# Two-layer spatial CNN scan: another order of two late phases, with new queues for their transfers, and shorter hand-overs from row scans to column scans

## The chip, the cores and the metric

The kernel runs on one core of a Trainium2 chip. A core has TensorE (PE, matmuls), VectorE (DVE), ScalarE (ACT), GpSimd (POOL) and SyncE (SP), which work from queues of their own, and 16 DMA engines that move data between DRAM and on-chip memory (SBUF). DMAs are issued from SP's, ScalarE's or GpSimd's queue. The metric is the time of one execution in microseconds.

## The reference

The input `x` is 32 images of 48 channels, 64 rows and 128 columns, float32. Two layers follow each other, each with its own weights; a layer normalizes, scans in four directions and adds the result to its input:

```python
def f(carry, inp):                    # one scan step; w: 48 x 48 x 5 taps
    nxt = inp + _conv1d(carry, w, b)  # convolution along the line
    return (nxt, nxt)
...
# down over the 64 rows, then up, then right over the 128 columns, then left,
# each direction on the output of the one before
...
x = x + _L0_conv_ref(_gn(x), ...)     # _gn: group norm, 16 groups of channels
x = x + _L1_conv_ref(_gn(x), ...)
```

The down and up scans use the same weights. Every step needs the step before, so a scan over rows is a chain of 63 steps in each direction, and one over columns a chain of 127.

## The kernel before, in words

The 32 images are four groups of 8 (`GB`). Row scans take one group at a time, column scans a pair of groups. So there are twelve phases, in the order of the tuple `PHASES`: `("rows", layer, group)` is a down and an up scan, `("cols", layer, pair)` a right and a left scan. The trace names the matmuls of a scan by layer, number and direction: `step_01u` is layer 0, group 1, up; `step_10r` is layer 1, pair 0, right. This text uses the same names. Before, layer 1 ends with the rows of groups 1, 2 and 3, then the columns of pair 0, then those of pair 1.

A step (`step`, matmuls at L741, VectorE's at L750) is 9 float32 matmuls into PSUM, and 3 VectorE instructions that add the bias and the step's input line and write the new line into SBUF, where the next step's matmuls read it.

SBUF holds three slots. A row phase has its 64 rows in them in two halves (`row_views`). A column phase has four quarters of 32 columns each, which share the slots (`slots`, `quarter`): the first is written out to `spill` after the right scan has passed it and the fourth takes its place; the left scan gets it back later. A quarter is six units (`UNITS`): three blocks of channels times the two groups of the pair. The scans' layouts differ, rows with whole lines in the free dimension and columns with blocks of 8 rows or columns (`E8`), so between them data pass through DRAM, in `ups`, called `upa` for layer 0 and `upb` for layer 1 in the trace.

What surrounds the steps is an agenda: `at(t, fn, ...)` puts a function at a step number, and the functions are traced in the order of these numbers. `in_order` keeps each engine's instructions in that order; nothing else paces them, so a transfer leaves as soon as its queue reaches it and what it waits for is done. `t0` is a phase's first step, `left` the start of its left scan, `end` its last step. The parts that matter here:

- `move_rows` writes finished rows to `ups` in blocks of 8 rows, ten DMAs for each (L231 is the common line of all DMAs), and loads a row phase's input from `source` (`mid` for layer 1) in four chunks of 16 rows, 20 DMAs each, on SP's queue. `scale_rows` (L614) then applies the normalization to a chunk with 24 ScalarE activations.
- `follows(k)` says that a column phase starts right after the rows of the second group of its own pair. Before, that holds for pairs 0 and 1 of layer 0. At such a seam the first quarter's units of that group are loaded on GpSimd's queue in pieces as its rows become ready: the blocks of rows from 32 on, then 16 to 31, 8 to 15, and at last rows 0 to 7. `move_rows` cuts the last block into rows 2 to 7 and rows 0 and 1. `hold_queues` makes SP's queue (by a tiny DMA into `pin`) and ScalarE's (by a copy) wait for the second column, before they load the second quarter.
- In the left scan each unit of a finished quarter goes through `load_residual`, `add_residual` (GpSimd, L673), for layer 1 `permute_unit` (L698, 3 copies on GpSimd and 5 on ScalarE for one unit), and then out. Layer 1's residual loads are on ScalarE's queue, into four tiles of `stage` and, for pair 0, one spare tile.
- Pair 1 of layer 1, the last phase, stores its results into `out` with `store_result`. So does pair 0 with the fourth quarter. The quarters named in `HELD` go to DRAM tiles `held` as one large DMA per unit instead (`hold_result`), and `let_result` copies them from there to `out` during the last phase, DRAM to DRAM, 48 results in 60 DMAs, on SP's queue.

The lines of the agenda that set the results' hand-over and the residual loads' queue, before:

```python
at(end + 63 + 1.9 * n, let_result, *what)
...
dma(nat[p0 : p0 + c1 - c0], by_col(t, e, j)[c0:c1], nc.scalar if layer else None)
```

Of the kernel before, what the change touches and what calls it, by code (L numbers as in the profile page):

```python
# [29 lines left out]
F32 = mybir.dt.float32  # L30
# [12 lines left out]
GB = 8  # L43
E8 = 8
FULL = 128
NG = E8 * C // FULL
NQ = 4
# [3 lines left out]
PIECES = (  # L51
    (0, 0, 48, 0, 0),
    (1, 0, 48, 0, 48),
    (2, 0, 32, 0, 96),
    (2, 32, 48, 1, 0),
    (3, 0, 48, 1, 16),
    (4, 0, 48, 1, 64),
    (5, 0, 16, 1, 112),
    (6, 0, 48, 2, 0),
# [19 lines left out]
def weight_runs():  # L79
# [24 lines left out]
PHASES = (  # L104
    ("rows", 0, 0),
    ("rows", 0, 1),
    ("cols", 0, 0),
    ("rows", 0, 2),
    ("rows", 1, 0),
    ("rows", 0, 3),  # L110
    ("cols", 0, 1),
    ("rows", 1, 1),
    ("rows", 1, 2),
    ("rows", 1, 3),
    ("cols", 1, 0),
    ("cols", 1, 1),
)

# [2 lines left out]
def kernel(  # L121
# [8 lines left out]
    nc = tc.nc  # L130
    B, _, H, W = x.shape
    NK = W // E8
    NH = H // E8
    KQ = NK // NQ
    WQ = W // NQ
    N = NK * GB
    RUN = KQ * GB
# [5 lines left out]
    BN = 512  # L143
# [8 lines left out]
    dram = ctx.enter_context(tc.tile_pool(name="dram", bufs=1, space=bass.MemoryType.DRAM))  # L152
# [19 lines left out]
    spare_tiles = [early[:, i * UNIT : (i + 1) * UNIT] for i in range(2)]  # L172
# [12 lines left out]
    junk = early[:, 3 * WEIGHTS + NG * N :]  # L185
# [15 lines left out]
        dram.tile([2 * NG, FULL, UNIT], F32, tag=f"spill{i}", name=f"spill{i}")  # L201
        for i in range(4)
    ]
    pin = dram.tile([FULL, 1], F32, tag="pin", name="pin")


    HELD = (2, 1, 0)
    held = {
        (j, half): dram.tile([NG, FULL, UNIT], F32, tag=f"held{j}{half}", name=f"held{j}{half}")
        for j in HELD  # L210
        for half in range(2)
    }

    def by_row(t, e, h0, h1):


        t = t.rearrange("c (i q a e n) -> e a c i q n", i=E8, q=NQ, a=NH, e=E8)[e, h0 // E8]
        return t[:, h0 % E8 : h0 % E8 + h1 - h0].rearrange("c i q n -> c (i q) n")

    def lines(t, h0, h1):  # L220

# [3 lines left out]
    def by_col(t, e, j):  # L225


        return t.rearrange("c (i q n) -> i q c n", i=E8, q=NQ)[e, j]

    def dma(dst, src, queue=None):  # L230
        (queue or nc.sync).dma_start(dst, src)  # L231

    tail = {}

    def in_order(fn, *args):


        traced = nc.cur_bb.bb.instructions
        n = len(traced)
        fn(*args)  # L240
        for ins in traced[n:]:
            if ins.engine in tail:
                tc.add_manual_dep(
                    ins,
                    tail[ins.engine].name,
                    mybir.DependencyInfo(
                        mybir.DependencyClass.NoSync, mybir.DependencyReason.DATA
                    ),
                    reason="in_order",
                )  # L250
            tail[ins.engine] = ins

    def pieces(o):
# [332 lines left out]
    def row(k, h):  # L586
        return row_views(k)[h // HALF][:, :, h % HALF]

    def move_rows(k, h0, h1, to_dram):

        _, layer, g = PHASES[k]
        view = row_views(k)[h0 // HALF]
        t = (ups if to_dram else source)[layer][g]
        for h in range(h0, h1, E8):
            end = min(h1, h + E8)
            for o in range(NG):
                for e, c0, c1, p0 in pieces(o):
                    here = view[p0 : p0 + c1 - c0, o, h % HALF : h % HALF + end - h]
                    here = here.rearrange("p h (q n) -> p (h q) n", q=NQ)
                    there = by_row(t, e, h, end)[c0:c1]  # L600
                    if to_dram:
                        dma(there, here)
                    else:
                        dma(here, there)
# [23 lines left out]
    UNITS = [(g, half) for g in range(NG) for half in range(2)]  # L628

    def quarter(k, j):  # L630
        return slot[slots(k)[j % 3]].rearrange("p (o s n) -> p s o n", s=2, o=NG)
# [13 lines left out]
                queue,  # L645
            )

    def hold_queues(k):

        done = quarter(k, 0)[:, 0, 0, RUN : RUN + 1]  # L650
        dma(pin, done)
        nc.scalar.copy(junk[:, BN - 1 :], done)

    def spill_unit(k, i, back):
        _, layer, pair = PHASES[k]
# [7 lines left out]
    def load_residual(k, j, i, nat):  # L663
        _, layer, pair = PHASES[k]
        o, half = UNITS[i]
        t = source[layer][2 * pair + half]
        for e, c0, c1, p0 in pieces(o):
            dma(nat[p0 : p0 + c1 - c0], by_col(t, e, j)[c0:c1], nc.scalar if layer else None)

    def add_residual(k, j, i, nat, eng=nc.gpsimd):  # L670
        o, half = UNITS[i]
# [28 lines left out]
    def in_output(j, g, e):  # L700


        t = out[g * GB : (g + 1) * GB].rearrange("b c (a e) w -> e (c a) b w", e=E8)
        return t[e, :, :, j * WQ : (j + 1) * WQ]
# [9 lines left out]

    def hold_result(j, i, perm):
        o, half = UNITS[i]
        dma(held[j, half][o], perm, nc.scalar)

    def let_result(j, half, e):

        src = held[j, half].rearrange("o p (a b n) -> (o p a) b n", a=NH, b=GB)
        for n, c0, c1, g, p0 in PIECES:
            if n == e:
                at = (g * FULL + p0) * NH
                dma(in_output(j, half, e)[c0 * NH : c1 * NH], src[at : at + (c1 - c0) * NH])


    def step(key, weights, b_at, src, inp, dst, whole, part):
# [91 lines left out]
    def at(t, fn, *args):  # L820
        agenda.append((t, len(agenda), fn, args))
# [31 lines left out]
    def plan_rows(k, t0, prev):  # L853
        if k == 1:
            ahead, scaled = (-34, -18, -3, 12), (-12, -2, 17, 33)
        elif prev == "cols":
            ahead, scaled = (-28, -12, 4, 20), (-13, 3, 19, 35)
        else:
            ahead, scaled = (-54, -43, 0, 11), (-22, -8, 16, 30)
        if k:  # L860
            for i in range(4):
                at(t0 + ahead[i], move_rows, k, i * LOAD, (i + 1) * LOAD, False)
                at(t0 + scaled[i], scale_rows, k, i * LOAD, (i + 1) * LOAD)

        cuts = list(range(0, H + 1, E8))
        following = PHASES[k + 1][0] == "cols"
        if following and follows(k + 1):
            cuts = [0, E8 // 4] + cuts[1:]
        for h0, h1 in zip(cuts, cuts[1:]):
            t = t0 + 2 * (H - 1) - h0  # L870
            if k == 0:
                t += 16 if h0 >= HALF else 68
            elif not following:
                t = t0 + 92 + 5 * (H - h1) / E8 + (34 if h1 <= HALF else 0)
            at(t, move_rows, k, h0, h1, True)
        at(
            t0 + H - 1,
            nc.gpsimd.tensor_copy,
            last.rearrange("p (o n) -> p o n", o=NG),
            row(k, H - 1),  # L880
        )

    def follows(k):

        _, layer, pair = PHASES[k]
        return PHASES[k - 1] == ("rows", layer, 2 * pair + 1)

    def plan_cols(k, t0, prev):
        _, layer, pair = PHASES[k]
        n = 2 * NG  # L890
        after = prev == "cols"
        if follows(k):
            at(t0 + 1.2, hold_queues, k)
        for i in range(n):
            if follows(k) and UNITS[i][1] == 1:
                other = nc.gpsimd
                at(t0 - 31 + i, load_unit, k, 0, i, 4, NH, 0, E8, other)
                at(t0 - 13 + i, load_unit, k, 0, i, 2, 4, 0, E8, other)
                at(t0 - 6 + i / n, load_unit, k, 0, i, 1, 2, 0, E8, other)
                at(t0 - 1.5, load_unit, k, 0, i, 0, 1, E8 // 4, E8, other)  # L900
                at(t0, load_unit, k, 0, i, 0, 1, 0, E8 // 4, other)
            else:
                early = 30 if after else 46 if k == 2 else 70
                at(t0 - early + 2 * i, load_unit, k, 0, i)
            if follows(k):
                queue = nc.scalar if i % 2 else nc.sync
                at(t0 + 1.5, load_unit, k, 1, i, 0, NH, 0, E8, queue)
            else:
                at(t0 + (3 if after else -24 + 2 * i), load_unit, k, 1, i)
            at(t0 + (38 if after else 8) + 2 * i, load_unit, k, 2, i)  # L910
            at(t0 + 33 + 2 * i, spill_unit, k, i, False)
            at(t0 + 50 + 2 * i, load_unit, k, 3, i)
        final = k == len(PHASES) - 1
        left = t0 + W - 1
        end = left + W - 1
        for i in range(n):

            t = left + 64 + 2 * i if layer == 0 else left + 39.5 + 4.5 * i
# [8 lines left out]
        if layer == 0:  # L927
            stats = ResultStatsV(f"r{2 * pair}"), ResultStatsA(f"r{2 * pair + 1}")
        tiles = [stage[:, i] for i in range(4)]
        if layer:  # L930
            tiles += spare_tiles[0 : 2 if final else 1]
        n = len(tiles)
        direct = [u for u in units if not (final and u[1] == 0)]

        for u, (t, j, i) in enumerate(direct):
            nat = tiles[u % n]
            o, half = UNITS[i]
# [26 lines left out]
        if layer == 0:  # L964
            t = units[-1][0] + 14
# [6 lines left out]
        if layer and not final:  # L972
            todo = [(j, half, e) for j in HELD for half in range(2) for e in range(E8)]
            for n, what in enumerate(todo):
                at(end + 63 + 1.9 * n, let_result, *what)
        if final:
            at(end + 4, last_results, k)

# [23 lines left out]
    tiles = [stage[0:PX, i] for i in range(4)]  # L1002
# [140 lines left out]
    done = 0  # L1143
# [65 lines left out]
```

## Time and profile before

| | us |
|---|---|
| median of three runs | 4292.32 (4289.52 to 4297.63) |
| the profiled execution | 4290.3 |
| its span in the profile | 4288.2 |
| TensorE busy | 4058.9 (95%) |
| VectorE busy | 2164.5 (50%) |
| ScalarE busy | 1340.1 (31%) |
| GpSimd busy | 886.2 (21%) |
| first step of a scan | 107.8 |
| last step of a scan ends | 4207.7 |
| granted TensorE clock, mean | 0.981 |

The profile is one execution, taken apart: busy time by engine, 40 slices of the span, the waits of each engine with what ended them, the timeline of instructions and of DMA issues, and windows, which give every engine's busy time in a stretch together with TensorE's granted clock (1.00 is full speed), the mean busy share of the 16 DMA engines and the rate in GB/s. Times in the profile count from the start of the span. A queue's name ends in q: SPq is SP's DMA queue. A row of a DMA queue shows when the issues ran, not when the data landed; the landing is given apart, as a time from issue.

### The profile page before, as it was taken

The numbers are of one execution on the slowest core, as the hardware profiler recorded it, in microseconds if no ns is written. First come the engines' busy times: TensorE is split into PE (matmuls) and PEld (weight loads), VectorE is DVE, ScalarE is ACT, GpSimd is POOL, SyncE is SP. The second block draws the span as 40 slices with busy tenths as digits, with TensorE's granted clock in tenths as the row PEclk, the third lists the DMA queues.
The fourth block names the chain that finished last, engine by engine and source line by source line (L and its number), as shares of the span: only waits on it lengthen the run. The fifth ranks groups of instructions, "written<-read, shape, count | busy, mean of one in ns | idle before, by whom it ended". The sixth has DMA issues, their size and how long they took to land. (4 is left out here: it accounts for less than half of the span.)

```text
span 4288.2 us, 89979 instructions
## 1 busy us (share of the span) xinstructions
PE 4058.9 (95%) x36648; PEld 4029.3 (94%) x36648; DVE 2164.5 (50%) x6503; ACT 1340.1 (31%) x2662; POOL 886.2 (21%) x906
## 2 busy tenths in 40 slices
PE   3699998999999999998999999999999999999992
PEld 1699998999999999998999999999999999999992
DVE  6345444446664444444446654444444444444443
ACT  1584301435793564100006772613000002210122
POOL 4271001325323020010005310000000024510352
PEclk9899999999999999999999999999999999999996
DMA  9599799857998979679308979939289049999999
GB/s 213 113 216 162 105 167 168 245 127 213 230 198 156 163 140 160 103 127 206 85 1 242 222 154 149 148 50 161 43 140 200 1 78 247 247 243 156 180 202 182
DMA packets 2116733, 680.12 MB, mean 159 GB/s; under 512 B 2005440, under 2 KB 2056160, under 8 KB 2076384
## 3 DMA queue, kind: packets, MB, share of 16 engines
q1 hardware_dynamic: 2015904, 581.64, 70.2%
q10 hardware_dynamic: 97216, 86.44, 9.9%
q0 software_dynamic: 3200, 6.30, 0.5%
q8 instruction: 288, 4.72, 0.5%
q14 instruction: 125, 1.02, 0.1%
HBM read 397.38 MB, written 295.98 MB: 162 GB/s over the span
## 5 line engine op out<-in xcount | busy, mean ns | idle before, releaser
L614 ACT ACTIVATE arena<-arena,offset,scale 128x256 f32<-128x256 f32 (+2 forms) x816 | 575.6, 801 | 432.9 <-DMA arena<-mid 176.1
L673 POOL TENSOR_TENSOR arena<-arena 128x2048 f32<-128x2048 f32 x80 | 363.1, 4553 | 1386.0 <-PE step_10l L741 434.1
L569 POOL COPY arena<-arena 96x256 f32<-96x256 f32 x448 | 265.0, 650 | 553.8 <-DMA arena<-in_x 444.2
L512 ACT ACTIVATE early<-arena 128x256 f32<-128x256 f32 x192 | 129.4, 674 | 477.2 <-POOL arena L673 471.2
L741 PE MATMUL step_00r<-arena,early 128*128 128x128 f32 x2286 | 251.5, 274 | 14.1 <-DMA arena<-upa 14.1
L741 PEld LDWEIGHTS step_00r<-arena,early 128*128 128x128 f32 x2286 | 251.1, 185 | 14.5 <-issue 14.4
L741 PE MATMUL step_01r<-arena,early 128*128 128x128 f32 x2286 | 250.6, 273 | 14.4 <-DMA arena<-upa 14.4
L741 PEld LDWEIGHTS step_01r<-arena,early 128*128 128x128 f32 x2286 | 250.4, 185 | 14.6 <-issue 14.5
L741 PE MATMUL step_11r<-arena,early 128*128 128x128 f32 x2286 | 251.3, 273 | 8.2 <-DVE arena L750 8.2
L741 PEld LDWEIGHTS step_11r<-arena,early 128*128 128x128 f32 x2286 | 250.8, 185 | 8.7 <-DVE arena L750 8.6
L741 PE MATMUL step_00l<-arena,wleft 128*128 128x128 f32 x2286 | 249.1, 272 | 0.0
L741 PEld LDWEIGHTS step_00l<-arena,wleft 128*128 128x128 f32 x2286 | 248.6, 184 | 0.0
L741 PE MATMUL step_10l<-arena,wleft 128*128 128x128 f32 x2286 | 248.5, 272 | 0.0
L741 PE MATMUL step_11l<-arena,wleft 128*128 128x128 f32 x2286 | 248.5, 272 | 0.0
L741 PE MATMUL step_01l<-arena,wleft 128*128 128x128 f32 x2286 | 248.4, 272 | 0.0
L741 PE MATMUL step_10r<-arena,early 128*128 128x128 f32 x2286 | 248.4, 272 | 0.0
L741 PEld LDWEIGHTS step_10l<-arena,wleft 128*128 128x128 f32 x2286 | 248.4, 184 | 0.0
L741 PEld LDWEIGHTS step_11l<-arena,wleft 128*128 128x128 f32 x2286 | 248.4, 184 | 0.0
L741 PEld LDWEIGHTS step_01l<-arena,wleft 128*128 128x128 f32 x2286 | 248.4, 184 | 0.0
L741 PEld LDWEIGHTS step_10r<-arena,early 128*128 128x128 f32 x2286 | 248.4, 184 | 0.0
L698 ACT COPY arena<-arena 128x256 f32<-128x256 f32 x172 | 99.7, 656 | 411.5 <-POOL arena L673 162.2
L240 ACT COPY early<-arena 128x1 f32<-128x1 f32 x2 | 0.4, 191 | 657.9 <-DVE arena L750 657.9
(189 smaller groups left out, 7171.3 us busy)
## 6 DMA issues: line engine op xcount, KB each, us to landing
arena<-in_x SPq DMA_DIRECT2D x24, 1536.0 KB, 11.6
xin<-arena SPq DMA_DIRECT2D x96, 384.0 KB, 4.7
arena<-xin SPq DMA_DIRECT2D x96, 384.0 KB, 8.5
mid<-arena SPq DMA_DIRECT2D x96, 384.0 KB, 7.8
arena<-mid SPq DMA_DIRECT2D x192, 192.0 KB, 4.2
upb<-arena SPq DMA_DIRECT2D x192, 192.0 KB, 3.9
arena<-upb SPq DMA_DIRECT2D x96, 384.0 KB, 12.3
arena<-xin SPq DMA_DIRECT2D x186, 192.0 KB, 4.3
```

The lines of the kernel that those rows point to most:

```text
L240: fn(*args)
L512: nc.scalar.activation(junk[:, 0:n], view[:, b], AF.Identity, accum_out=self.sum[:, i, j : j + 1])
L569: copy(dst[:, r, q], src[:, r0 + r, q])
L614: nc.scalar.activation(args[0], args[0], AF.Identity, bias=args[2], scale=args[1])
L673: eng.tensor_tensor(unit, unit, nat, ALU.add)
L698: copy(by_w(perm)[:, a], src[:, a])
L741: nc.tensor.matmul(part(whole(ps[o])[0:m], -s), weights[:, i, at : at + m], part(src(i), s), start=seen[o] == 1, stop=seen[o] == left[o],)
```

## The change

The rows of group 3 of layer 1 move between the columns of pair 0 and pair 1. With that, pair 1's column phase follows its own group's rows, so `follows` holds for it too, as a third seam.

All four quarters of pair 0's results now go to `held`, on SP's queue rather than ScalarE's. Its residual loads are on SP's queue too, into four tiles rather than five. `let_result`, for 64 results, moves to ScalarE's queue: 30 results during group 3's rows, 34 during pair 1's right scan, each behind `pace`, a ScalarE copy of one column that reads the result of a given scan step.

At the seams, rows 8 to 15 are written to DRAM with their first quarter of columns alone, ten DMAs of 48 partitions or fewer. Rows 0 to 7 do not go through DRAM for the first quarter: `send_row` copies them within SBUF from the row layout into the column layout, 94 small DMAs, taken by ScalarE's and SP's queues in turn. Columns 0 to 3 of each block of 8 (`e` below) leave as each row is done, columns 4 to 7 after the last row. The other three quarters of rows 0 to 15 are written to DRAM after the end, in 60 DMAs. The pin is gone, and only ScalarE's queue waits for the second column. The second quarter's loads change queues: the second group's go from ScalarE's to SP's, the first group's from SP's to ScalarE's.

```diff
     ("rows", 1, 1),
     ("rows", 1, 2),
+    ("cols", 1, 0),
     ("rows", 1, 3),
-    ("cols", 1, 0),
     ("cols", 1, 1),
...
-    HELD = (2, 1, 0)
+    HELD = (3, 2, 1, 0)
...
+    def send_row(k, h, wanted):
+        here = row(k - 1, h)
+        for e, c0, c1, o, p0 in PIECES:
+            if e not in wanted:
+                continue
+            for i, d0, d1, to, q0 in PIECES:
+                a, b = max(c0, d0), min(c1, d1)
+                if i != h or a >= b:
+                    continue
+                turns[0] += 1
+                dma(
+                    quarter(k, 0)[q0 + a - d0 : q0 + b - d0, 1, to, e * RUN : (e + 1) * RUN],
+                    here[p0 + a - c0 : p0 + b - c0, o, 0:RUN],
+                    nc.scalar if turns[0] % 2 else nc.sync,
+                )
+    def send_rest(k, wanted):
+        for e in wanted:
+            for h in range(E8 - 1, -1, -1):
+                send_row(k, h, (e,))
+    together += [send_row, send_rest]
-    def hold_queues(k):
-        done = quarter(k, 0)[:, 0, 0, RUN : RUN + 1]
-        dma(pin, done)
-        nc.scalar.copy(junk[:, BN - 1 :], done)
+    def hold_queue(k):
+        nc.scalar.copy(junk[:, BN - 1 :], quarter(k, 0)[:, 0, 0, RUN : RUN + 1])
...
     def hold_result(j, i, perm):
         o, half = UNITS[i]
-        dma(held[j, half][o], perm, nc.scalar)
+        dma(held[j, half][o], perm)
...
-                dma(in_output(j, half, e)[c0 * NH : c1 * NH], src[at : at + (c1 - c0) * NH])
+                dst = in_output(j, half, e)[c0 * NH : c1 * NH]
+                dma(dst, src[at : at + (c1 - c0) * NH], nc.scalar)
+    def pace(k, n):
+        if PHASES[k][0] == "rows":
+            done = row(k, n + 1 if n < H - 1 else 2 * H - 3 - n)[:, 0, 0:1]
+        else:
+            kb, e = divmod(n + 1, E8)
+            j, kk = divmod(kb, KQ)
+            done = quarter(k, j)[:, 0, 0, e * RUN + kk * GB :][:, 0:1]
+        nc.scalar.copy(junk[:, BN - 1 :], done)
...
-        if following and follows(k + 1):
-            cuts = [0, E8 // 4] + cuts[1:]
+        seam = following and follows(k + 1)
+        if seam:
+            cuts = cuts[2:]
+            end = t0 + 2 * (H - 1)
+            at(end - E8, move_rows, k, E8, 2 * E8, True, 0)
+            for h in range(E8 - 1, -1, -1):
+                at(end - h, send_row, k + 1, h, range(0, E8 // 2))
+            at(end, send_rest, k + 1, range(E8 // 2, E8))
+            for q in range(1, NQ):
+                at(end + 0.1 if q == 1 else end + 1.6, move_rows, k, 0, 2 * E8, True, q)
...
-                at(t0 - 1.5, load_unit, k, 0, i, 0, 1, E8 // 4, E8, other)
-                at(t0, load_unit, k, 0, i, 0, 1, 0, E8 // 4, other)
...
-                queue = nc.scalar if i % 2 else nc.sync
+                queue = nc.sync if UNITS[i][1] else nc.scalar
                 at(t0 + 1.5, load_unit, k, 1, i, 0, NH, 0, E8, queue)
...
-        if layer:
-            tiles += spare_tiles[0 : 2 if final else 1]
+        if final:
+            tiles += spare_tiles
...
-                at(end + 63 + 1.9 * n, let_result, *what)
+                if n < 30:
+                    m = 48 + int(2.3 * n)
+                    at(end + m, pace, k + 1, m - 2)
+                    at(end + m, let_result, *what)
+                else:
+                    m = 36 + int(2.6 * (n - 30))
+                    at(end + 2 * (H - 1) + m, pace, k + 2, m - 2)
+                    at(end + 2 * (H - 1) + m, let_result, *what)
```

`load_residual` takes ScalarE's queue in the last phase alone. `together` keeps the sends of the two queues in the order in which they were written.

More of the change, by code (lines that the diff above doesn't have):

```diff
@@ L203 @@
     ]
-    pin = dram.tile([FULL, 1], F32, tag="pin", name="pin")
-    HELD = (2, 1, 0)
+    HELD = (3, 2, 1, 0)
     held = {
@@ L212, with by_row @@
     }
-    def by_row(t, e, h0, h1):
+    def by_row(t, e, h0, h1, q):
         t = t.rearrange("c (i q a e n) -> e a c i q n", i=E8, q=NQ, a=NH, e=E8)[e, h0 // E8]
-        return t[:, h0 % E8 : h0 % E8 + h1 - h0].rearrange("c i q n -> c (i q) n")
+        t = t[:, h0 % E8 : h0 % E8 + h1 - h0]
+        return t.rearrange("c i q n -> c (i q) n") if q is None else t[:, :, q]
     def lines(t, h0, h1):
@@ L233 @@
     tail = {}
+    queues = (nc.sync.engine, nc.scalar.engine)
+    together = []
     def in_order(fn, *args):
@@ L250, in in_order @@
                 )
+            if ins.engine in queues and "DMA" in ins.opcode:
+                if fn in together and "queue" in tail:
+                    tc.add_manual_dep(
+                        ins,
+                        tail["queue"].name,
+                        mybir.DependencyInfo(
+                            mybir.DependencyClass.NoSync, mybir.DependencyReason.DATA
+                        ),
+                        reason="together",
+                    )
+                tail["queue"] = ins
             tail[ins.engine] = ins
@@ L587, in row, with move_rows @@
         return row_views(k)[h // HALF][:, :, h % HALF]
-    def move_rows(k, h0, h1, to_dram):
+    def move_rows(k, h0, h1, to_dram, q=None):
         _, layer, g = PHASES[k]
@@ L598, in move_rows @@
                     here = view[p0 : p0 + c1 - c0, o, h % HALF : h % HALF + end - h]
-                    here = here.rearrange("p h (q n) -> p (h q) n", q=NQ)
-                    there = by_row(t, e, h, end)[c0:c1]
+                    there = by_row(t, e, h, end, q)[c0:c1]
+                    if q is None:
+                        here = here.rearrange("p h (q n) -> p (h q) n", q=NQ)
+                    else:
+                        here = here[:, :, q * RUN : (q + 1) * RUN]
                     if to_dram:
@@ L646, in load_unit @@
             )
-    def hold_queues(k):
-        done = quarter(k, 0)[:, 0, 0, RUN : RUN + 1]
-        dma(pin, done)
-        nc.scalar.copy(junk[:, BN - 1 :], done)
+    turns = [0]
+    def send_row(k, h, wanted):
[12 more added lines that the diff above has]
+                    nc.scalar if turns[0] % 2 else nc.sync,
+                )
+    def send_rest(k, wanted):
[5 more added lines that the diff above has]
+        nc.scalar.copy(junk[:, BN - 1 :], quarter(k, 0)[:, 0, 0, RUN : RUN + 1])
     def spill_unit(k, i, back):
@@ L667, in load_residual @@
         for e, c0, c1, p0 in pieces(o):
-            dma(nat[p0 : p0 + c1 - c0], by_col(t, e, j)[c0:c1], nc.scalar if layer else None)
+            dma(nat[p0 : p0 + c1 - c0], by_col(t, e, j)[c0:c1], nc.scalar if k == len(PHASES) - 1 else None)
     def add_residual(k, j, i, nat, eng=nc.gpsimd):
@@ L892, in plan_cols @@
         if follows(k):
-            at(t0 + 1.2, hold_queues, k)
+            at(t0 + 1.2, hold_queue, k)
         for i in range(n):
@@ L974, in plan_cols @@
             for n, what in enumerate(todo):
-                at(end + 63 + 1.9 * n, let_result, *what)
+                if n < 30:
+                    m = 48 + int(2.3 * n)
+                    at(end + m, pace, k + 1, m - 2)
+                    at(end + m, let_result, *what)
+                else:
+                    m = 36 + int(2.6 * (n - 30))
+                    at(end + 2 * (H - 1) + m, pace, k + 2, m - 2)
+                    at(end + 2 * (H - 1) + m, let_result, *what)
         if final:
```

## The prediction

> **What bounds the kernel now.** I read the page first, then the TensorE waits, then the timeline and the windows of every place where TensorE stands still.
>
> ```profile
> PE 4058.9 (95%) x36648; PEld 4029.3 (94%) x36648; DVE 2164.5 (50%) x6503; ACT 1340.1 (31%) x2662; POOL 886.2 (21%) x906
> ...
> PEclk9899999999999999999999999999999999999996
> DMA  9599799857998979679308979939289049999999
> ```
>
> TensorE is the bound: a chain of scan steps, nearly always at full clock. A group's 63 row steps take 124.3 us where nothing disturbs them (1.97 a step), a pair's 127 column steps 248.3 us (1.955). The change does not touch a step. It can only move what lies between steps, so I list the excess over these clean lengths, read from each phase's first and last matmul: 14.4 at the seam from group 1's up scan (01u) into pair 0's right scan (00r) and 3.1 in 00r; 14.7 and 2.2 at the seam 03u into 01r; 10.0 in 11d, 2.8 in 02d; 11.1 in 11r; 0.0 to 0.2 in 13d, 13u, 10r and 10l. The waits name the causes:
>
> ```profile
> PE step_01r L741 <- DMA arena<-upa: 14.4, 1, 14.4
> PE step_00r L741 <- DMA arena<-upa: 14.1, 1, 14.1
> PE step_11r L741 <- DVE arena L750: 8.2, 1, 8.2
> PE step_11d L741 <- DVE arena L750: 3.3, 1, 3.3
> ```
>
> The first seam, in the timeline:
>
> ```profile
> 649.58 10.02 SPq L231 DMA_DIRECT2D upa<-arena  x16
> ...
> 657.50 3.94 POOL L231 DMA_DIRECT2D arena<-upa  x8 [3.22 <-DMA upa<-arena]
> 662.19 1.00 POOL L231 DMA_DIRECT2D arena<-upa  x2 [0.74 <-issue]
> 665.29 3.05 PE L741 MATMUL step_00r<-arena,early 128*128 128x128 f32 x12 [14.10 <-DMA arena<-upa]
> ```
>
> The last row ends at 651.2; it is written to DRAM, and only then loaded back on GpSimd's queue. The third wait, and the price of standing still, in windows (column 2 is the length, the third number from the end the granted clock, then DMA share and GB/s):
>
> ```profile
> 665.00:671.00 6.00, 5.71 (x27) 5.58 (x27) 1.05 (x3) 0.19 (x1) 0.00 (x0) 0.50 0.73 21
> 2442.00:2576.00 134.00, 129.00 (x1146) 128.34 (x1145) 77.19 (x243) 100.72 (x190) 29.64 (x9) 0.97 0.83 161
> 3700.00:3959.00 259.00, 250.75 (x2285) 250.32 (x2284) 122.11 (x381) 23.15 (x40) 49.47 (x32) 0.98 0.96 209
> 3834.00:3838.00 4.00, 4.00 (x19) 4.00 (x20) 1.17 (x4) 0.00 (x0) 0.00 (x0) 0.50 0.93 201
> ```
>
> After 14.1 us of idling the next 6 us run at half clock, after 8.25 us more than 4; that costs 2 to 3 us on top. Gaps of 1.0 to 1.2 us (1262.7, 2505.8) drew none.
>
> **Short seams, pairs of layer 0.** Removed: DRAM write and reload of rows 0 to 7's first quarter, and the pin. Added: 94 small SBUF-to-SBUF DMAs. Six or so per row leave while later rows compute; row 0's wait for its last VectorE result, and step 1 then needs an issue (0.30 to 0.5 us) and a landing (small DMAs: 1.7 to 2.2 us in the quiet part of this seam, 2.5 to 3.9 in its loaded part). That makes 2 to 3 us, and a gap of 2.5 at 125.5 drew 3.4 us at half clock, 1.7 lost; I take 3.5. The 47 DMAs for columns 4 to 7 leave after the end, on two queues: at 2.1 us a landing with eight in flight (the program makes each DMA of these two queues wait for the landing of the one eight before it, and the trace shows it: the issue after the pin's landing at 676.40 starts at 676.42) 47 need 12.4 us, so column 7 is there at about 15 to 16 us, and its step comes at 3.5 + 7 x 1.955 = 17.2. Close; at 3.2 us a landing it is 19, late by 2 or 3. Two seams: 34.4 now, 7 afterwards, **-27.4** (ends -31 and -16).
>
> **A third seam.** Pair 1 of layer 1 now follows its own group's rows; before, its right scan began with its data loaded. **+3.5** (1.5 to 17).
>
> **Later quarters behind the seams.** 60 writes of 48 KB and the sends now stand ahead of the second quarter's loads on SP, ScalarE's half behind the sends. Before, these loads ran from 668.8 to 719.8, 51 us, and were due at 665.3 + 32 x 1.955 = 727.9. Now they start some 14 us after the rows' end, take 51, and share the engines with 1 MB of writes first (8 us at these loads' own 6.3 MB in 51 us): 65 to 73 us after the end, due at 66. So 0 to 7 late, with a part of a clock penalty; I take 2 at each of three seams, **+6** (0 to 20).
>
> **Group 3's rows after pair 0's columns.** 13d had no excess, since its neighbours were rows. Now it starts like 02d and 11d, the two rows phases after columns (2.8 and 10.0). What it needs are four row chunks into slots that the results leave, and ScalarE's scaling:
>
> ```profile
> 2420.34 23.46 SPq L231 DMA_DIRECT2D arena<-mid  x20
> ...
> 2460.64 25.98 SPq L231 DMA_DIRECT2D arena<-mid  x20
> ...
> 2497.51 26.07 SPq L231 DMA_DIRECT2D arena<-mid  x20
> ```
>
> A chunk holds SP for about 25 us, and ScalarE then for 18 to 24 (24 activations of 0.75 to 0.84, L614). In 11d the fourth was about 5 us late. For 13d the change puts pair 0's residual loads on SP, with four tiles in place of five, and its 1 MB result writes too; in the built order two to four of these stand between every two chunks. Each load there waits for a sum (4.55 us on GpSimd, L673), permuting (2.9 us, L698) and a write of about 12 us. I get the fourth chunk in at 70 us into the phase, ScalarE busy with the third until then, so scaled at 70 + 36 = 106; row 48 is due at 47 x 1.973 = 93. That is 13 late and 3 of clock, **+16**; ends 3 (as 02d) and 25.
>
> **Handing over pair 0's results.** 64 instead of 48 results, on ScalarE's queue, 30 of them in 13d/13u, 34 in 11r, each behind a copy that waits for a scan step. On ScalarE's queue nothing urgent stands behind them there. But SP shares the eight-deep chain. In the built order, SP's last third-quarter load waits for a handover paced by step 63, and step 64 needs that load: 0.4 us for copy and issue, 6.7 us for the handover's landing (its row in the page), 0.1, and 5 to 9 for the load, 14 in all, of which 2 are the step: 11.5 plus 2.9 of clock = 14.4. At step 96 the same with a handover paced by step 92: about 6.5 + 2. Together 23, where 11r loses 11.1 now: **+12**. Ends: -11, if SP is well ahead of that order and nothing is late, and +20, at double landing times. The Trainium skill ("DMA: Bandwidth & Descriptors", "Issuing engines are not separate DMA queues") says that DMAs from different engines interleave on the same 16 engines, so that another issuer only saves issue time. By it the move to ScalarE's queue would be worth nothing, and this term would be 0 at best. The trace's DMA share of 0.96 over 11r agrees with no spare room.
>
> **The rest.** Pair 1's left scan and the 80.5 us after the last step (4207.7 to 4288.2) keep their transfers in the same order, at a DMA share of 1.1 to 1.3: 0 (within 4). The handovers that leave 11r's end are done before it.
>
> Sum: -27.4 + 3.5 + 6 + 16 + 12 = **+10.1**. The profiled execution took 4290.3 us (span 4288.2 and 2.1 around it), 2.0 under the median of 4292.3; added to the median this gives 4302.4.
>
> **Rivals.**
> 1. *Faster: the shares are covered.* 13d loses as little as 02d (2.8), 11r loses nothing, no quarter is late: -27.4 + 3.5 + 2.8 - 11.1 = -32, 4260. For it: 02d, and 11r's wait came from traffic that is now spread over 13d and 13u as well, where the DMA row has a slice at 2 tenths. Against: the paced handovers stand in the load's own chain.
> 2. *Slower: the wait moves into 13d and 11r in full.* One mechanism: DMAs held in order behind a late landing. It decides from the point at which a chunk stands behind two result writes of over 12 us. 25 + 20 + 12 + 3.5 - 27.4 = +33, 4325.
> 3. *The seams do not get shorter*, because the small DMAs land at 4 us under the preceding writes (DMA share 0.98 in 01u): 17 at each of three seams, +17 + 6 + 16 + 12 = +51, 4343. Against: the writes just before shrink to a quarter.
>
> **How the numbers follow.** Forecast 0.42 (own range 4288 to 4318), rival 1 0.22, rival 2 0.18, rival 3 0.08; 0.10 for mixtures, nearly all of them with only one of the two new waits, so 4270 to 4285. A measurement here can tell 0.2%, 8.6 us. Faster: rival 1 and most mixtures, 0.30. Same: the forecast's lower part and the last mixtures, 0.20. Slower: the rest, 0.50. The range 4258 to 4332 leaves out half of rival 1, rival 3 and a third of rival 2.
>
> **What would show it.** Right: gaps of 2 to 5 us before step_00r, step_01r and step_11r's first matmuls; a wait of 10 us or more on L614 in step_13d near row 48; step_11r stopping at columns 64 and 96 on loads of upb. Wrong: 13d clean and 11r without a gap (rival 1); first-step gaps of 10 us and over (rival 3); or a tail that is not 80 us, which no part of my sum covers.

## The result, and the profile after

The changed kernel takes 4395.97 us, median of 4 runs (4386.05 to 4400.78), against 4290.92 (4278.85 to 4297.63) for the kernel before on the same chip: 1.024 times as long, 95% interval 1.0225 to 1.0256. That is slower by some 105 us, where +10 was forecast and the range ended at 4332.

The profiled execution has a span of 4391.9 us, 103.7 more. From the page and the waits of TensorE:

```profile
PE 4077.6 (93%) x36648; PEld 4044.6 (92%) x36648; DVE 2167.8 (49%) x6503; ACT 1350.8 (31%) x2727; POOL 896.7 (20%) x916
...
PEclk9899999999999999999999999999999999899996
```

```profile
PE step_11r L793 <- DMA arena<-arena: 33.6, 2, 31.5
...
PE step_11r L793 <- DVE arena L802: 25.0, 3, 15.7
PE step_13d L793 <- DVE arena L802: 24.7, 4, 20.3
PE step_00r L793 <- DMA xin<-arena: 10.5, 1, 10.5
PE step_01r L793 <- DMA arena<-arena: 6.4, 1, 6.4
PE step_13d L793 <- issue: 5.7, 2, 5.0
PE step_00r L793 <- DMA arena<-arena: 5.5, 1, 5.5
```

TensorE's busy time grew by 18.7 us (the same 36648 matmuls, more of them at half clock); the rest is waiting. The steps are the same (L741 is L793 now). The excess over the clean lengths of the phases, in microseconds, tells where, and the same count is used for the experiments below:

| | seams 01u, 00r, 03u, 01r | 10l + 13d | 13u with the third seam | 11r | after the last step |
|---|---|---|---|---|---|
| before | 34.4 | 0.2 | 0.2 | 11.1 | 80.5 |
| after | 34.5 | 38.7 | 31.8 | 35.9 | 88.0 |
| difference | +0.1 | +38.5 | +31.6 | +24.8 | +7.5 |

The five differences make 102.5 of the 103.7. Each has its rows in the trace.

**The first seam.** ScalarE's and SP's queues (start, length, count of issues):

```profile
638.07 33.26 ACTq L231 DMA_DIRECT2D arena<-arena  x47
```

```profile
639.63 32.01 SPq L231 DMA_DIRECT2D arena<-arena  x47
671.68 13.96 SPq L231 DMA_DIRECT2D upa<-arena  x20
691.04 13.41 SPq L231 DMA_DIRECT2D arena<-upa  x10
704.79 28.80 SPq L231 DMA_DIRECT2D upa<-arena  x40
...
821.86 24.20 SPq L231 DMA_DIRECT2D arena<-upa  x17
```

The 94 sends leave one after the other in turn, one per 0.32 us, 0.6 us of each queue. They begin 12.4 us before the rows' end at 650.5. When the last row's result is written, at 650.9, 33 of the first 47 have left; the 47th leaves at 655.2, and the first step comes at 656.1, after 5.55 us. Then SP writes: 20 issues in 14.0 us, and behind the second quarter's loads 40 in 28.8 us. The fourth quarter's last 17 loads stand behind all that, at 821.9. Before, they were issued from 796.6 on:

```profile
796.62 26.60 SPq L231 DMA_DIRECT2D arena<-upa  x17
```

In the changed kernel the last of them lands at 858.1, before at 832.2. VectorE waits for it to add column 96 (TensorE's row above names another transfer that landed at the same time):

```profile
858.29 0.61 DVE L802 SCALAR_TENSOR_TENSOR arena<-step_00r,bd,arena 128x128 f32<-128x128 f32 x2 [10.79 <-DMA arena<-upa]
```

**13d.** The timeline ahead of row 48, first SP's queue with the fourth chunk and the loads behind it:

```profile
3512.77 34.18 SPq L231 DMA_DIRECT2D arena<-mid  x24
...
3551.65 1.44 SPq L231 DMA_DIRECT2D arena<-mid  x3
```

then GpSimd's sum and ScalarE (at the end of a row, the idle time before it and what ended it):

```profile
3558.33 4.51 POOL L714 TENSOR_TENSOR arena<-arena 128x2048 f32<-128x2048 f32 x1 [22.05 <-PE step_13d L793]
```

```profile
3562.88 2.82 ACT L739 COPY arena<-arena 128x256 f32<-128x256 f32 x5 [25.56 <-POOL arena L714]
3565.61 14.12 ACT L630 ACTIVATE arena<-arena,offset,scale 128x256 f32<-128x256 f32 x19
```

The fourth chunk's last load lands at 3550.5. ScalarE does not scale it, since a permute comes first in its queue; it had been idle for 25.56 us for GpSimd's sum, and that for a residual load that stood behind the chunk on SP (issued at 3548 to 3551, landed at 3558.1, 0.25 us before the sum starts; the row of the sum names TensorE). The scaling starts 15 us late at 3565.6, and TensorE stands still for 20.26 us.

**The third seam and 11r.** SP's row writes before the seam, and the hand-overs on ScalarE's queue:

```profile
3657.31 97.88 SPq L231 DMA_DIRECT2D upb<-arena  x55
3755.28 32.17 SPq L231 DMA_DIRECT2D arena<-arena  x47
```

```profile
3705.43 0.19 ACT L777 COPY early<-arena 128x1 f32<-128x1 f32 x1 [5.73 <-DVE arena L802]
3705.45 0.54 ACTq L231 DMA_DIRECT2D out<-held  x1
```

55 writes took SP 97.9 us. The trace gives the landings: the hand-over issued at 3705.45 lands at 3710.49, and SP's next write is issued at 3710.51, after one at 3704.12. Of the 48 us in which SP's queue issued nothing between 3655 and 3740 (stops of over 0.3 us), 40 ended within 0.06 us of the landing of a hand-over. At the rows' end, 3739.4, SP still had 19 row writes to issue. The sends begin at 3752.9, 13.5 us after the rows' end, where at the first seam they began 12.4 us ahead of it: 26 us later, and the seam's gap of 31.55 us is 26 us longer than the 5.55 there. In 11r the third quarter's loads then come as the prediction said, behind the last paced hand-over:

```profile
3829.89 37.86 SPq L231 DMA_DIRECT2D upb<-arena  x29
3867.86 47.95 SPq L231 DMA_DIRECT2D arena<-upb  x20
```

and VectorE's timeline at column 64:

```profile
3920.64 0.61 DVE L802 SCALAR_TENSOR_TENSOR arena<-step_11r,bd,arena 128x128 f32<-128x128 f32 x2 [15.99 <-DMA arena<-upb]
```

The hand-over issued at 3902.76, after step 63, lands at 3915.03; SP's next load is issued at 3915.05, the last at 3915.39, and that lands at 3920.52. At column 96 it is the same: hand-over landed at 3984.17, SP's issue at 3984.19, last load landed at 3992.25. TensorE stops for 15.7 and 7.1 us, and for 2.0 and 2.2 us before columns 7 and 8, for late sends. The pacing holds SP as well: it issued nothing from 3835.1 to 3852.45, since the next hand-over in the chain waited for its scan step, left at 3848.01 and landed at 3852.43.

### The profile page after: what moved, and what is told of

It reads as the page before. It is cut to its first block, busy times and chain, and to the rows that moved or that the text cites. A ratio compares the mean times of both kernels' runs of the same rounds, so it can differ in the third digit from the quotient of the medians.

```text
span 4391.9 us, 90829 instructions
## 1 busy us (share of the span) xinstructions
PE 4077.6 (93%) x36648; PEld 4044.6 (92%) x36648; DVE 2167.8 (49%) x6503; ACT 1350.8 (31%) x2727; POOL 896.7 (20%) x916
## 5 line engine op out<-in xcount | busy, mean ns | idle before, releaser
L714 POOL TENSOR_TENSOR arena<-arena 128x2048 f32<-128x2048 f32 x84 | 381.2, 4552 | 1567.3 <-PE step_10l L793 460.8
L793 PE MATMUL step_11r<-arena,early 128*128 128x128 f32 x2286 | 257.2, 277 | 58.6 <-DMA arena<-arena 33.6
L793 PEld LDWEIGHTS step_11r<-arena,early 128*128 128x128 f32 x2286 | 256.1, 188 | 59.7 <-issue 31.7
L793 PE MATMUL step_00r<-arena,early 128*128 128x128 f32 x2286 | 254.3, 275 | 16.6 <-DMA xin<-arena 10.5
L793 PEld LDWEIGHTS step_00r<-arena,early 128*128 128x128 f32 x2286 | 253.3, 187 | 17.6 <-DVE arena L802 11.7
L793 PE MATMUL step_01r<-arena,early 128*128 128x128 f32 x2286 | 251.8, 274 | 8.1 <-DMA arena<-arena 6.4
L793 PEld LDWEIGHTS step_01r<-arena,early 128*128 128x128 f32 x2286 | 251.2, 185 | 8.7 <-issue 6.8
L793 PE MATMUL step_00l<-arena,wleft 128*128 128x128 f32 x2286 | 249.1, 272 | 0.0
L793 PE MATMUL step_10l<-arena,wleft 128*128 128x128 f32 x2286 | 248.8, 272 | 0.1
L793 PE MATMUL step_11l<-arena,wleft 128*128 128x128 f32 x2286 | 248.7, 272 | 0.1
L793 PEld LDWEIGHTS step_10l<-arena,wleft 128*128 128x128 f32 x2286 | 248.5, 184 | 0.3 <-DVE arena L802 0.3
L793 PEld LDWEIGHTS step_11l<-arena,wleft 128*128 128x128 f32 x2286 | 248.5, 184 | 0.3 <-DVE arena L802 0.3
L793 PEld LDWEIGHTS step_00l<-arena,wleft 128*128 128x128 f32 x2286 | 248.6, 184 | 0.0
L793 PE MATMUL step_01l<-arena,wleft 128*128 128x128 f32 x2286 | 248.4, 272 | 0.0
L793 PE MATMUL step_10r<-arena,early 128*128 128x128 f32 x2286 | 248.4, 272 | 0.0
L793 PEld LDWEIGHTS step_01l<-arena,wleft 128*128 128x128 f32 x2286 | 248.4, 184 | 0.0
L793 PEld LDWEIGHTS step_10r<-arena,early 128*128 128x128 f32 x2286 | 248.4, 184 | 0.0
L739 ACT COPY arena<-arena 128x256 f32<-128x256 f32 x192 | 110.6, 653 | 396.7 <-POOL arena L714 269.7
L802 DVE SCALAR_TENSOR_TENSOR arena<-step_11r,bd,arena 128x128 f32<-128x128 f32 x381 | 122.3, 348 | 193.5 <-PE step_11r L793 126.1
```

The source lines that it names most:

```text
L714: eng.tensor_tensor(unit, unit, nat, ALU.add)
L739: copy(by_w(perm)[:, a], src[:, a])
L793: nc.tensor.matmul(part(whole(ps[o])[0:m], -s), weights[:, i, at : at + m], part(src(i), s), start=seen[o] == 1, stop=seen[o] == left[o],)
L802: nc.vector.scalar_tensor_tensor(dst(o), whole(ps[o]), bd[:, o, layer, way : way + 1], inp(o), ALU.add, ALU.add,)
```

## The experiments

Times are given against runs of the kernel before on the same chip; its medians there were 4300.74 us beside `seams_alone`, `order_alone`, `lets_pool` and `res_act`, 4301.01 beside `perm_pool`, `lets_early`, `seams_pool` and `new_best`, and 4299.64 beside the other three. Gaps are from one profile each; the same code shows the gap at column 96 of 00r anywhere between 5.8 and 14.5 us in seven of these profiles, so a few microseconds at one place decide nothing. `perm_pool` and `no_pace` were run twice each, the others four to eleven times.

**Which part loses: `seams_alone` and `order_alone`.** The two halves of the change, each on the kernel before.

```diff
 # seams_alone: the changed kernel, with these as before
-    ("cols", 1, 0),
     ("rows", 1, 3),
+    ("cols", 1, 0),
-    HELD = (3, 2, 1, 0)
+    HELD = (2, 1, 0)
...   residual loads and hold_result on ScalarE's queue, let_result on SP's, unpaced
 # order_alone: the kernel before, with everything of the change but the short seams
```

> The kernel before with the short seams alone (two of them, since the order of the phases stays). First theory, shares of the loss add up by place: the seams' gaps shrink from 14.1 and 14.4 us to about 6 each, as in the changed kernel, but the 60 small writes put 25 us onto SP's queue ahead of the later quarters, so 00r waits some 10 us at column 96; together within 5 us of the kernel before, about 4291. Second theory, the seams gain and only the new order loses: 4270 or less.

4300.20 us, ratio 1.0001 (0.9986 to 1.0015): no difference. The gaps at the two seams are 5.7 and 6.4 us, column 96 of 00r waits 5.8, 01r waits 4.1 before column 8, and the four phases have an excess of 32.8 where the kernel before has 34.4. So the short seams shorten the seams and give it back within the next 200 us.

> The new order with the queues and the paced hand-over, and the seams of before in all three places. First theory: the first two seams and 00r as in the kernel before; 13d loses its 35 to 40 us as in the changed kernel, 11r its two waits at columns 64 and 96, and the third seam costs 14 us plus what SP is behind, 25 to 35: about 4380 to 4400. Second theory, the loss at the end comes from the short seam's 94 sends and 60 writes: the third seam at 14 to 17 and 11r near 15, about 4350.

4370.72 us, 1.017 (1.0145 to 1.0195), less than expected. 13d is as in the changed kernel (10l and 13d 38.2), and the seam is worse:

```profile
PE step_11r L752 <- DMA arena<-upb: 39.7, 1, 39.7
```

But 11r has an excess of 3.1 us only, which the expectation had missed. There the third quarter's loads do not stand behind 60 writes and come early enough. The waits at columns 64 and 96 need both halves of the change: writes that push SP's loads back, and hand-overs for them to be late behind.

**What holds SP: `lets_pool`, `lets_early` and `no_pace`.**

```diff
 # lets_pool
-                dma(dst, src[at : at + (c1 - c0) * NH], nc.scalar)
+                dma(dst, src[at : at + (c1 - c0) * NH], nc.gpsimd)
...
-        nc.scalar.copy(junk[:, BN - 1 :], done)
+        nc.gpsimd.tensor_copy(junk[:, BN - 2 : BN - 1], done)
 # lets_early: lets_pool, and
-                if n < 30:
+                if n < 16:
...
-                    m = 36 + int(2.6 * (n - 30))
+                    m = 36 + int(1.75 * (n - 16))
 # no_pace: the changed kernel without both calls of pace
```

> The changed kernel with the hand-over of pair 0's results and its pacing on GpSimd's queue, nothing else. First theory, the paced hand-overs hold SP through the eight-deep chain of landings that the two queues share: 11r's waits at columns 64 and 96 (15.7 and 7.1 us) go, and SP's row writes before the third seam are on time, so its 31.6 us fall to 10 or less; 13d stays; about 4340. Second theory, the DMA engines are simply full: the same bytes at the same steps give the same waits, 4385 to 4400.

4345.21 us, 1.0114 (1.0083 to 1.0145). 11r's excess falls from 35.9 to 4.2, the third seam's gap from 31.6 to 16.4:

```profile
PE step_13d L793 <- DVE arena L802: 22.4, 4, 16.7
PE step_11r L793 <- DMA arena<-arena: 16.4, 1, 16.4
```

The same bytes, at the same steps, cost some 50 us less in a queue that does not share SP's chain of landings. In 11r the engines were not full: in the changed kernel their share was 0.80 at 132 GB/s between 3830 and 3905, ahead of column 64. Ahead of the third seam they were (1.09 between 3640 and 3740, and 1.10 here). What differs there is SP's queue: with `lets_pool` it has no stop of over 0.3 us between two issues in that stretch, though a single issue takes up to 12.8 us.

One thing besides the queue changed too, the packets in which the copies travel (packets, MB and share of the engines' time for ScalarE's queue, q10, and GpSimd's, q0; first the changed kernel, then `lets_pool`):

```profile
q10 hardware_dynamic: 295520, 71.31, 10.3%
q0 software_dynamic: 3840, 8.26, 0.7%
...
q10 hardware_dynamic: 97632, 46.14, 6.0%
q0 software_dynamic: 11264, 33.43, 3.2%
```

The 25.2 MB of the hand-over went from 127 bytes a packet to 3.4 KB, and from 4.3% of the engines' time to 2.5%. That this relief made the gain is unlikely, since nothing lands sooner: the hand-overs take 7.2 us (median; 6.4 in the changed kernel), SP's row writes ahead of the third seam 5.6 (5.1), its loads in 11r 11.9 (7.2). What share it has of the 50 us no run separates.

> The changed kernel with the hand-over on GpSimd's queue, and 16 of the 64 results passed on in 13d and 13u (none in the last 40 steps), 48 in 11r. First theory, what is left of the third seam's loss (16.4 us) is SP's row writes landing late, 12 to 18 us each, beside a bunch of ten hand-overs: the gap falls to 6 or 7, as at the first two seams, and the time by about 10 from that of the hand-over on GpSimd's queue alone. Second theory, SP is late by its own writes: the gap stays above 13.

4349.07 us, 1.0108 (1.009 to 1.0127). The gap at the third seam falls to 5.8, as at the other two, so the bunch of hand-overs beside the last row writes was what was left of it. The time did not follow, and 10 us less were expected. In its profile 00r, 11r, 13d and 10d have 3 to 9 us more each than with `lets_pool`; for 11r more hand-overs there may explain it, for 00r and 10d, far ahead of the edit, nothing does but the spread between executions.

> The changed kernel without the pacing copies: the hand-overs on ScalarE's queue leave as soon as the queue reaches them. First theory, what holds SP is a landing that cannot come before a scan step: without it 11r's waits at columns 64 and 96 go or fall below 6 us, and the third seam falls from 31.6 to 10 or less, since the first 30 hand-overs are through long before the seam; about 4345. Second theory, sharing the eight-deep chain with DRAM-to-DRAM copies is what costs, paced or not: the gaps move but their sum stays above 40 us, 4375 or more.

4412.97 us, 1.026 (1.0241 to 1.0279): no faster than the changed kernel (whether slower, the intervals, which overlap, do not tell), and the first theory falls. The seam's gap does fall, to 22.2 us, but 11r pays, in TensorE's waits, and SP's and ScalarE's queues show with what:

```profile
PE step_11r L793 <- DVE arena L802: 56.7, 4, 21.3
...
PE step_11r L793 <- DMA arena<-arena: 22.2, 1, 22.2
```

```profile
3854.99 64.47 SPq L231 DMA_DIRECT2D upb<-arena  x40
```

```profile
3801.85 105.79 ACTq L231 DMA_DIRECT2D out<-held  x42
```

42 DMAs of the hand-over in a row hold ScalarE's queue for 105.8 us, and SP's 40 writes in the same chain take 64.5, 1.6 us each, where 40 of them took 28.8 in 00r. What costs is that SP shares the chain with copies that land a median of 7.0 us after their issue here, where its own 40 writes land after 3.6; the pacing decides where the loss falls, and without it the loss is not smaller.

**13d: `res_act` and `perm_pool`.**

```diff
 # res_act
-            dma(..., nc.scalar if k == len(PHASES) - 1 else None)
+            dma(..., nc.scalar if layer else None)
 # perm_pool: pair 0's last quarter of results in layer 1 is permuted on GpSimd alone
-                at(t + 2.5, permute_unit, k, j, i, nat, (nc.gpsimd, nc.scalar, nc.scalar))
+                at(t + 2.5, permute_unit, k, j, i, nat, (nc.gpsimd,) if j == 0 and not final else ...)
```

> The changed kernel with pair 0's residual loads of layer 1 back on ScalarE's queue, four tiles. First theory, 13d's wait of 20 us at row 48 comes from a residual load that stands behind a row chunk on SP, and ScalarE's scaling in its queue behind that unit's permuting: the loads no longer stand behind the chunks, the wait falls below 10 us, 4375 to 4385. Second theory, the results themselves (sum, permuting, 12 us write, four tiles) set the time at which the fourth chunk comes: 13d unchanged, 4390 to 4400.

4385.54 us, 1.0207 (1.0177 to 1.0236). 10l and 13d have 21.6 instead of 38.7, and 13d's longest gap is 7.0. Against the changed kernel's 1.024 that is some 14 us, close to the 17 of that place. The two intervals overlap, so it is the place that shows the gain, and not the total.

> The changed kernel, with the permuting of pair 0's last quarter of results in layer 1 on GpSimd alone (8 copies there, none on ScalarE). First theory, the scaling of 13d's fourth chunk stands on ScalarE behind a permute whose residual load stands on SP behind that very chunk: the chunk lands 15 us before the scaling starts, so 13d's gap of 20.3 us falls to 4 to 9 and the time by about 13, to 4380. Second theory, the chunk itself is late and ScalarE merely follows: gap 17 to 21, no difference in time.

4382.39 us, 1.0189 (1.0166 to 1.0212), as the first theory has it. The gap at row 48 falls from 20.3 to 3.9 us, and nothing else was touched but where the copies of six units run (8 a unit; 30 of the 48 move from ScalarE to GpSimd):

```profile
PE step_13d L793 <- DVE arena L802: 8.7, 4, 3.9
```

The two remedies of one chain agree: each breaks it at another link (the load behind the chunk, the scaling behind the permute).

**Short seams that do not push: `seams_pool`.**

```diff
 # seams_pool: seams_alone, and
-                at(end - h, send_row, k + 1, h, range(0, E8 // 2))
-            at(end, send_rest, k + 1, range(E8 // 2, E8))
+                at(end - h, send_row, k + 1, h, range(0, 3))
+            at(end, send_rest, k + 1, range(3, E8))
...   send_rest takes SP's, ScalarE's and GpSimd's queue in turn
-                        dma(there, here)
+                        dma(there, here, nc.gpsimd if q in (2, 3) else None)
```

> The kernel before with other short seams alone: columns 0 to 2 of each block of 8 are sent as the rows are done, columns 3 to 7 after the end on three queues (GpSimd's as well), and the 40 writes of the third and fourth quarter are on GpSimd's queue. First theory, two alternating queues send one row piece per 0.32 us whatever they wait for, and SP's 60 writes at 0.49 us push the later quarters: the seams' gaps fall from 5.7 and 6.4 to about 3, the waits at column 96 of 00r (5.8) and column 8 of 01r (4.1) go, 12 to 22 us under the kernel before. Second theory, the later waits come from the DMA engines being full after a seam: gaps at column 96 and 8 stay, within 6 us of the kernel before.

4276.08 us, 0.9945 (0.9931 to 0.9959): 24 us under the kernel before, and the fastest of all. SP issues the fourth quarter's last 17 loads from 793.5 on, where it was 821.9 in the changed kernel. The gaps are 3.2 and 4.5 us, and the later ones are gone:

```profile
PE step_11r L793 <- DVE arena L802: 8.2, 1, 8.2
...
PE step_01r L793 <- DMA arena<-arena: 4.5, 1, 4.5
...
PE step_00r L793 <- DMA arena<-arena: 3.2, 1, 3.2
```

The four phases' excess is 13.0, where both the kernel before and the changed one have 34.

**All remedies: `new_best`, `new_perm2`, `new_res_pool`.** `new_best` is the changed kernel with `lets_early`, `perm_pool` and the edits of `seams_pool`. The other two go on from it: `new_perm2` permutes the last two quarters on GpSimd (`j <= 1`), `new_res_pool` has pair 0's residual loads in layer 1 on GpSimd's queue.

> The changed kernel with all remedies: hand-over on GpSimd's queue and early, last permutes on GpSimd, sends and late writes also on GpSimd's queue. First theory: 45 to 50 us off by the hand-over, 10 by its being early, 12 by the permutes, 15 to 20 by the seams: about 4305, still above the kernel before, since 13d keeps waits of some 15 us that its rows did not have there. Second theory, the remedies collide on GpSimd's queue: above 4330.

4295.75 us, 0.9987 (0.9976 to 0.9997): over 100 us back, and a hair under the kernel before. The remedies add up. By place: seams 13.2, 10l and 13d 17.9, third seam 5.1, 11r 1.9. Against `seams_pool` the new order saves 10 us in 11r and pays 23 in 13d and at a third seam.

> The kernel with all remedies, and the permuting of pair 0's last two quarters of results (before: the last one) on GpSimd alone. First theory, the scalings of 13d's first and second chunk still stand behind such permutes on ScalarE: 13d's gaps of 4.0 and 3.7 us at its start and at row 16 shrink to below 2, and with the clock 8 to 14 us go: 4285 where the kernel before takes 4300. Second theory, the chunks are late on SP themselves: no difference.

4300.78 us, 1.0004 (0.9995 to 1.0013): no gain. The gap at 13d's start goes (10l from 4.3 to 0.1), ScalarE is idle whenever a chunk's last load lands, but 14.6 us appear at row 32. There the chunks are late on SP, as the second theory has it.

> The kernel with all remedies, and pair 0's residual loads of layer 1 on GpSimd's queue, so that SP has result writes and row chunks alone there. First theory, chunks and residual loads no longer delay each other: 13d's gaps at its start and at row 16 below 2 us, 8 to 14 us less in all. Second theory, GpSimd's sums now wait behind loads that wait for a tile: results later, 13d's waits 10 us or more longer.

4316.63 us, 1.0033 (1.002 to 1.0045), longer. 13d's start waits 13.0 us and row 32 10.6: GpSimd's loads wait for a tile (9.7 and 12.3 us for a result write), and its sums behind them.

## Why the prediction was wrong

The sum was +10, and the profiles differ by 103.7. Term by term it missed 10.8 us at the two seams, 10.7 behind them, 28.1 at the third seam, 22.5 in 13d, 12.8 in 11r and 7.5 after the last step. In most of these places the same thing failed: the term left out what else stood in the same queue or the same chain of landings.

**Short seams** (-27.4, which takes in the starts of 00r and 01r; measured -16.6 in 01u and 03u). The step that failed is "six or so per row leave while later rows compute". Both queues together issue one per 0.32 us, so six fill nearly the whole turn of a row (1.97 us), and the first ten, which took 5.0 us, are never made up for: 14 of the first 47 were still to leave when the last row was done. The 47 late ones were rightly said to be close: 1.7 us before column 8 of 01r.

**Later quarters** (+6, ends 0 and 20; measured +13.8 in 00r and +2.9 in 01r). I followed the second quarter alone, which was indeed in time. I also put all 60 writes ahead of its loads; 20 stand ahead and 40 behind. The 60 writes hold SP for 43 us (14.0 and 28.8), part of it waiting for landings, and the third and the fourth quarter with the group inputs between them move by as much as 25 us, where the fourth had 21 us to spare. `seams_alone` shows the price: it takes all that the seams gain.

**A third seam** (+3.5, end 17; measured +31.6). The failed step is the missing one: the seam was priced as a copy of the first, in a place where another part of the same change had the sends start 26 us later. `lets_pool` and `lets_early` bring it to 5.8. I had written of the shared chain under 11r and not asked who else is in it: the row writes that this very seam needs.

**13d** (+16, end 25; measured +38.5 with 5.5 in 10l). "The fourth chunk in at 70 us": it was in at 93. "Scaled at 70 + 36": ScalarE was taken to be busy; it was idle, and held by the order of its queue. The nearest rows (02d, 11d) have no permutes of the same results ahead of the scaling, so they bound nothing.

**11r** (+12; measured +24.8). The mechanism and its places were right, the waits at columns 64 and 96 were put at 11.5 and 6.5 us and are 15.7 and 7.1 (the first hand-over took 12.3 us to land, not 6.7). Missed were the late sends (4.2) and most of the half clock after the seam and the four stops (the excess of 35.9 less gaps of 27.1). The reason was half right: sharing counts, taking the pacing away alone wins nothing (`no_pace`), and without the 60 writes there is no wait at all (`order_alone`).

**The rule from the Trainium skill** ("DMA: Bandwidth & Descriptors", "Issuing engines are not separate DMA queues"), by which another issuer saves the issue time alone. In this program the issuer decided much more: the same hand-overs from GpSimd's queue took 1.2% off the time, and travelled in larger packets. The engines may well be shared as it says; the waits for landings that the program puts into SP's and ScalarE's queues are not a matter of the engines, and a rule on bandwidth does not price them.

**After the last step** (0 within 4; measured +7.5). This stays open. The transfers of the left scan are the same; over the experiments this stretch has 75.9 to 84.0 us, 80.7 and less in the old order and 81.9 and more in the new.

Rival 1 (-32) had only the shorter waits at the seams right; what they gained was given back, and 13d and 11r lost instead of being covered. Rival 2 named the class, DMAs held in order behind a late landing, and priced it by the nearest rows, +33 in all; it, too, had the third seam at 3.5, and 13d alone cost 38 where its end was 25.

## What to carry to other kernels

Before a transfer is moved to another queue or order, list every queue and chain of landings that it will stand in, and for each what stands behind it and when that is due; the cost of a move is at those places, not at its own. An issue has a price per piece: the writes that come with shortening a wait of 14 us filled the same queue for 43 us here and were paid for 200 us later. Where a loss may come from an order between queues, a change of the issuing engine, with bytes and times left as they are, helps to tell it from a lack of bandwidth; look at the packets and the landings as well, since the engine can change them.

## What was not expected of the hardware

A send of 128 bytes by 16 to 48 partitions and a write of 48 KB hold their queue nearly alike (0.60 and 0.49 to 0.72 us), and land after 1.7 us in a quiet stretch. Copies from DRAM to DRAM of up to 384 KB land after a median of 6.4 us in the changed kernel (2.8 to 15.8), and beside ten of them, in `lets_pool`, four row writes took 12 to 18 us, where the median there was 5.6. The same copies travel as packets of 127 bytes from ScalarE's queue and of 3.4 KB from GpSimd's.
